# One VectorE chunk instead of two in the layer norms of the first and last layers of an attention and FP4 feed-forward stack, with a new planned order

## The chip, the cores and the metric

The kernel runs on one core of a Trainium2 chip. The metric is device time in microseconds (us) for one execution, and smaller is better. The five engines of the core run side by side and meet at semaphores: TensorE (PE; the weight loads are shown apart as PEld), VectorE (DVE), ScalarE (ACT), GpSimd (POOL) and SyncE (SP), which issues the transfers. The reference is in float32 and so is every matmul of the kernel; a float32 matmul shows in the trace as two instructions.

## The reference

The input holds 8 batches of 1024 tokens with 128 features. Cut to what matters:

```python
mod = (silu(c) @ wmod).reshape(8, 6, 1, 128)         # sa, ca, ga, sb, cb, gb
h = layernorm(x) * (1 + ca) + sa
for i in range(6):                                   # DEPTH
    xn = layernorm(h, ln1_w[i], ln1_b[i])
    q, k, v = xn @ wq[i], xn @ wk[i], xn @ wv[i]     # 8 heads of 16
    q, k = softmax(q, over features), softmax(k, over tokens)
    h = q @ (k.T @ v) @ wo[i] + bo[i] + h
    xn = layernorm(h, ln2_w[i], ln2_b[i])
    h = leaky(xn @ w1[i], 0.01) @ w2[i] + h          # 128 -> 512 -> 128
x = x + ga * h
h = layernorm(x) * (1 + cb) + sb
gate, up = fp4(h) @ fp4(w_gate).T, fp4(h) @ fp4(w_up).T      # 352 wide
return x + gb * (fp4(silu(gate) * up) @ fp4(w_down).T)
```

`fp4` scales blocks of 16 by their largest magnitude and rounds them to a grid of eight magnitudes. There are thus 2 layer norms in each of 6 layers for each of 8 batches, and 2 more for each batch around them.

## The kernel before

**Tiling.** One batch is a tile of 128 partitions by 1024 columns: 8 chunks of 128 columns, each holding 128 tokens. Nearly every step works on a half (H = 2) of HC = 4 chunks. There are four lanes of buffers (LANES = 4). Batch b uses lane b % 4, so batches 0 to 3 start the kernel together and batches 4 to 7 follow as the lanes come free.

**A half layer norm** (`layernorm`, called once for each half) is this chain. DVE takes `bn_stats` of four chunks (line 641) and aggregates them (647). ACT takes a logarithm and an exponential (661, 666) for a first reciprocal root. DVE refines it and makes the shift in four small steps (671 to 687). Then the four chunks are normalised: DVE does HV chunks (`apply_v`, line 693: one subtract and multiply each) and ACT the other HC - HV (`apply_s`, line 700: one activation each). HV is 2 in all norms within the layers. PE then transposes the four chunks (line 719) and ACT moves the result out of PSUM with the norm's weight and bias (929). In tile names, `a` marks the norm ahead of the attention, `m` the one ahead of the 512 wide part, `i` the one ahead of the first layer and `f` the one ahead of the FP4 part. Both `i` and `f` are made by `modulated_norm`, which passes its own HV.

**The rest of a layer.** k matmuls (949) with a maximum on DVE (956) and exponentials on ACT (972); q matmuls (996) with softmax steps on DVE, ACT and POOL (1005 to 1037); transposes; the 128 by 128 context (1059 to 1100); the output matmuls (1126), added onto x by DVE (1111); then the `m` norm, the first wide matmul (1172), Prelu on ACT (1181) and the second wide matmul (1189). After six layers `ffn` makes the FP4 rounding (747 to 792), gate and up matmuls (1233), silu on ACT (1241), the product on DVE (1249), and `down` rounds that, transposes it (1289), multiplies (1313), adds onto x (1322) and stores.

**The order.** Nothing is issued in the order in which it is written. `add` puts each step into a list with its engine, its modelled duration, and what it reads and writes; from these come the dependences. `Plan.order` then plays the list through a model of the engines and of the 8 PSUM banks. At each turn it takes the step that can start soonest; among equals, the one with the longest modelled tail plus a lead. Leads come from `LEAD[b][i]` (batch b, stage i: 0 is the start, 1 to 6 the layers, 7 the FP4 part), and `TURNS` replaces single leads when the model's clock passes a given time. The resulting order is fixed on every engine, which takes its instructions one after another.

**Fillers.** Where the model sees PE idle for longer than GAP (0.35 us), it puts in 128 by 128 matmuls of the identity into a free bank (`warm`, line 1361) until BRINK (0.1 us) ahead of the next step. Until the model's time COLD (11.5 us) PE's work counts double, `mm(P)` being 0.223 us otherwise:

```python
cold = 2 if e == "PE" and free[e] < self.COLD else 1
gap = e == "PE" and t - free[e] > self.GAP / cold
while gap and min(bank_free) <= free[e]:
    to = free[e] + cold * mm(P)
    if to > t - self.BRINK:
        break
```

Of the kernel before, what the change touches and what calls it, by code (L numbers as in the profile page):

```python
# [14 lines left out]
P = 128  # L15
# [47 lines left out]
class Ps:  # L63


    n = 0
# [17 lines left out]
class Plan:  # L84
# [58 lines left out]
    def order(self, leads, turns, warm):  # L143


        steps = self.steps
        for s in steps:
            for d in s.deps:
                steps[d].outs.append(s.n)
        for s in reversed(steps):  # L150
            s.tail = s.occ + s.lat + max((steps[o].tail for o in s.outs), default=0.0)
        free = dict.fromkeys(self.LAT, 0.0)
        free["PE"] = 1.8
        bank_free = [0.0] * BANKS
        left = [len(s.deps) for s in steps]
        ready = [0.0] * len(steps)
        cand = {e: {s.n for s in steps if s.eng == e and not s.deps} for e in free}
        table, port_free, now = None, 0.0, 0.0
        leads, turns = [list(x) for x in leads], list(turns)
        out, todo = [], len(steps)  # L160
        while todo:
            while turns and turns[0][0] <= now:
                for b, i, lead in turns.pop(0)[1]:
                    leads[b][i] = lead
            banks = sorted(bank_free)
            best = None
            for e, c in cand.items():
                for n in c:
                    s = steps[n]
                    t = max(free[e], ready[n], port_free if s.port else 0.0)  # L170
                    need = sum(x.bank is None for x in s.ps)
                    if need:
                        t = max(t, banks[need - 1])
                    if t < INF:
                        cost = SWITCH if s.func and table and s.func != table else 0.0


                        lead = leads[s.stage[0]][s.stage[1]] if s.stage else s.lead
                        pick = (t + cost, -s.tail - lead, n, t, cost)
                        if best is None or pick < best[1]:  # L180
                            best = (e, pick)
            assert best is not None
            e, (_, _, n, t, cost) = best
            cold = 2 if e == "PE" and free[e] < self.COLD else 1
            gap = e == "PE" and t - free[e] > self.GAP / cold
            while gap and min(bank_free) <= free[e]:
                to = free[e] + cold * mm(P)
                if to > t - self.BRINK:
                    break
                w, bank = Step(), bank_free.index(min(bank_free))  # L190
                w.fn, w.func = lambda bank=bank: warm(bank), None
                free[e] = bank_free[bank] = to
                out.append(w)
            s, todo = steps[n], todo - 1
            cand[e].discard(n)
            now = t + cost
            end = now + s.occ * (2 if e == "PE" and now < self.COLD else 1)
            table = s.func or table
            port_free = end if s.port else port_free
            for x in s.ps:  # L200
                if x.bank is None:
                    x.bank = min(range(BANKS), key=lambda i: bank_free[i])
                    bank_free[x.bank] = INF
                x.users -= 1
                if x.users == 0:
                    bank_free[x.bank] = end + s.lat
            free[e] = end
            for o in s.outs:
                ready[o] = max(ready[o], end + s.lat + self.SEE[steps[o].eng])
                left[o] -= 1  # L210
                if left[o] == 0:
                    cand[steps[o].eng].add(o)
            out.append(s)
        return out
# [21 lines left out]
def mm(n):  # L236

    return 0.0115 + n * 1.654e-3
# [11 lines left out]
def kernel(  # L250
# [22 lines left out]
    B, T, D = x_d.shape  # L273
# [15 lines left out]


    LEAD = [
        [2405, 3996, 461, 247, -1202, -1296, -1300, -3196],
        [1413, 1593, 3441, 1928, -2207, 1189, 1781, -248],
        [366, -108, -1676, -2703, -3835, 1594, -2630, -2514],
        [-241, 558, -1413, 208, -413, 228, -5405, -156],
        [694, -3633, -2192, -2384, -870, -487, -1194, -1272],
        [-3687, 2479, 1403, 3083, -1193, -6, -811, -1034],
        [725, 1777, 204, -1637, -400, -327, -320, -670],
        [3404, 589, 1158, 1867, -7, -962, -419, -2719],
    ]  # L300

    TURNS = [
        (3, [(1, 0, -62)]),
        (27, [(3, 0, -535)]),
        (36, [(2, 1, -485)]),
        (39, [(3, 1, -531)]),
        (45, [(0, 2, 1516), (2, 1, -553)]),
        (48, [(2, 1, -544)]),
        (57, [(1, 1, 1518), (1, 2, 2846), (1, 3, 649)]),
        (75, [(1, 1, 1516)]),  # L310
        (90, [(1, 1, 773)]),
        (105, [(0, 3, 2919), (0, 4, 1470), (0, 5, 1376), (0, 7, -524)]),
        (120, [(0, 3, 2762), (2, 1, -721)]),
        (150, [(1, 2, -201)]),
        (165, [(2, 1, 797)]),
        (180, [(1, 2, 1215)]),
        (210, [(2, 2, 832)]),
        (225, [(3, 1, 914), (3, 6, -4315)]),
        (240, [(0, 5, 828)]),
        (255, [(0, 5, 2639), (0, 6, 2635)]),  # L320
        (270, [(2, 3, 156)]),
        (285, [(0, 7, 811), (1, 3, 64)]),
        (300, [(4, 0, -33)]),
        (315, [(2, 2, 1013), (4, 0, 939)]),
        (330, [(3, 2, 544)]),
        (345, [(0, 7, 348), (2, 3, -400)]),
        (360, [(0, 7, 811), (2, 3, 1746), (2, 4, -2375)]),
        (405, [(1, 4, -3784), (4, 1, -3690)]),
        (420, [(1, 4, -3786)]),
        (435, [(2, 4, -3941)]),  # L330
        (450, [(1, 4, -2313)]),
        (465, [(4, 1, -4514)]),
        (480, [(1, 5, 1477)]),
        (495, [(3, 5, 1525)]),
        (525, [(1, 5, 1515), (2, 5, 1254)]),
        (555, [(1, 7, 1337)]),
        (570, [(2, 5, 1311)]),
        (600, [(1, 7, 1342)]),
        (615, [(1, 7, 1337), (3, 6, -3519), (5, 2, 2464)]),
        (630, [(3, 7, 1425)]),  # L340
        (675, [(5, 1, 2181)]),
        (690, [(4, 1, -2521)]),
        (705, [(2, 7, -2804), (4, 2, -2786), (4, 3, -4487), (4, 7, -1958)]),
        (735, [(5, 2, 3162)]),
        (780, [(6, 1, 323)]),
        (795, [(2, 7, -2027)]),
        (810, [(3, 7, 2088), (5, 3, 1769)]),
        (825, [(4, 3, -2043)]),
        (840, [(5, 4, -2386), (7, 1, 210), (7, 2, 779)]),
        (870, [(4, 3, -2494)]),  # L350
        (885, [(7, 1, 493)]),
        (915, [(6, 2, 913)]),
        (930, [(4, 3, -1826), (4, 4, -1241)]),
        (945, [(5, 4, -2139), (5, 6, -1878)]),
        (975, [(6, 3, -2917)]),
        (1005, [(7, 4, -2167)]),
        (1020, [(5, 5, -1207)]),
        (1035, [(5, 5, -1166)]),
        (1065, [(7, 4, -1977)]),
        (1140, [(4, 6, -2161), (5, 6, -1912)]),  # L360
        (1155, [(4, 6, -1857)]),
        (1170, [(4, 7, -1928)]),
        (1245, [(5, 7, -1905)]),
        (1260, [(6, 7, -139)]),
        (1275, [(6, 6, -1635)]),
        (1305, [(5, 7, -1974), (7, 7, 205)]),
        (1320, [(6, 7, -143), (7, 6, -143)]),
        (1335, [(6, 7, 201)]),
        (1350, [(6, 7, 206), (7, 7, 207)]),
    ]  # L370
    LATE = 140.0
    NQ = 4
# [252 lines left out]
    def layernorm(ln, dst, src, h, n, HV=HC // 2):  # L625
# [72 lines left out]
        def apply_s():  # L698
# [6 lines left out]
        low, high = at(dst, h)  # L705
        add(
            "ACT", (HC - HV) * (act(D, 2) + 0.04), apply_s, r=[*at(src, h), shift, rstd],
            w=[high] if HV else [low, high],
        )
        if HV:  # L710
            add("DVE", HV * 0.256, apply_v, r=[*at(src, h), mv, rstd], w=[low], port=True)
# [205 lines left out]
            )  # L917


    def normed(ln, x, which, to, l, params, n):  # L920


        xh, xT = big(ln, which, f"xh_{n}"), big(ln, to, f"xT_{n}")
        for h in range(H):
            layernorm(ln, xh, x, h, n)
            t = transposed(xh, h)
            add(
                "ACT", act(HW, 2),
                lambda t=t, h=h: nc.scalar.activation(  # L929
                    half(xT, h), t.ap(), AF.Identity,  # L930
                    bias=col(params + 1, l), scale=col(params, l),
                ),
                r=[t, "cols"], w=at(xT, h),
            )
        return xh, xT

    def layer(x, b, l, ln, mod):
        n = f"{b}_{l}"
        xh, xT = normed(ln, x, "A", "B", l, 0, f"a{n}")

        nmax = Buf(lanes_p, [P, H + 1], f"nmax{ln}", f"nmax_{n}", H + 1)
        ksum = Buf(lanes_p, [P, H + 1], f"ksum{ln}", f"ksum_{n}", H + 1)
# [188 lines left out]
            add("PE", HC * mm(D), out_mm, r=[*at(qT, h), m], w=[to])  # L1131
            onto_x(to, h)

        _, xmT = normed(ln, x, "C", "A", l, 2, f"m{n}")
        if l == L - 1:


# [283 lines left out]
```

## Time and profile before

| | |
|---|---|
| median of 3 runs | 1401.61 us (1401.01 to 1402.49) |
| the profiled execution's own time | 1401.35 us |
| its span, first to last instruction | 1399.6 us |
| PE busy | 1387.0 us, 99% of the span; 21.0 us of it fillers |
| DVE busy | 1136.8 us, 81% |
| ACT busy | 967.7 us, 69% |
| POOL busy | 250.3 us, 18% |

The profile is one execution. The span leaves out what lies ahead of the first and behind the last instruction: 1401.35 - 1399.6 = 1.75 us. A busy PE includes fillers, which are there only because nothing else could run. The gap that matters is therefore PE's idle time and its fillers together: 1399.6 - 1387.0 + 21.0 = 33.6 us.

### The profile page before, as it was taken

The page shows a single profiled execution, that of the slowest core. Times are in us where ns is not written, and L with a number is a line of the kernel's source. Part 1 is how long each engine was busy: PE and PEld are TensorE (multiplying, and loading weights), DVE is VectorE, ACT ScalarE, POOL GpSimd, SP SyncE. Part 2 cuts the span into 40 slices and gives each one's busy share as a digit, 9 for nine tenths or more (in the row PEclk, how much of TensorE's full clock was granted, in tenths as well). Part 3 has the DMA queues.
Part 4 walks back from the last instruction along what each step waited for, and adds up shares of the span by engine and source line. Part 5 has one row for each costly group of instructions (what it writes and reads, how often), then busy time and mean ns, then how long its engine had stood idle before and what let it go on. Part 6 is the DMA issues. An engine that isn't in the chain of part 4 may idle for free. (4 is left out here: it accounts for less than half of the span.)

```text
span 1399.6 us, 26260 instructions
## 1 busy us (share of the span) xinstructions
PE 1387.0 (99%) x9149; PEld 1112.8 (80%) x9149; DVE 1136.8 (81%) x4504; ACT 967.7 (69%) x2284; POOL 250.3 (18%) x216
## 2 busy tenths in 40 slices
PE   8999999999999999999999999999999999999999
PEld 6779778877888887877787788787877887888877
DVE  8998747689878674999899999685767576899997
ACT  6786756676777765777768767676667667677674
POOL 2312000022201010223121241011011022222332
PEclk9999999999999999999999999999999999999999
DMA  7100000000000000000000000000000000000001
GB/s 219 48 1 1 1 1 1 1 17 12 16 1 1 1 1 1 16 13 18 30 12 13 0 31 1 1 1 1 1 1 1 1 1 1 2 1 1 16 8 38
DMA packets 16436, 18.77 MB, mean 13 GB/s; under 512 B 1600, under 2 KB 10536, under 8 KB 16304
## 3 DMA queue, kind: packets, MB, share of 16 engines
q1 hardware_dynamic: 16304, 17.10, 4.0%
q8 instruction: 72, 1.18, 0.4%
q14 instruction: 60, 0.49, 0.1%
HBM read 12.88 MB, written 4.22 MB: 12 GB/s over the span
## 5 line engine op out<-in xcount | busy, mean ns | idle before, releaser
L1172 PE MATMUL ps<-xT_m,w_sb 128*128 128x512 f32 x768 | 351.5, 593 | 1.3 <-ACT g L1241 0.9
L1172 PEld LDWEIGHTS ps<-xT_m,w_sb 128*128 128x128 f32 x768 | 136.3, 190 | 126.5 <-issue 90.4
L1037 POOL TENSOR_TENSOR q<-q,qsum 128x512 f32<-128x512 f32 x96 | 101.7, 1070 | 703.0 <-DVE qsum L1032 312.8
L1111 DVE TENSOR_TENSOR x<-ps,x 128x512 f32<-128x512 f32 x192 | 130.4, 683 | 111.8 <-PE ps L1189 96.5
L996 PEld LDWEIGHTS ps<-wq_sb,xT_a 128*128 128x128 f32 x768 | 96.3, 192 | 26.1 <-issue 16.5
L700 ACT ACTIVATE xh_a<-x,shift_a,rstd_a 128x128 f32<-128x128 f32 x192 | 83.3, 488 | 26.0 <-DVE shift_a L687 25.6
L1189 PEld LDWEIGHTS ps<-w_sb,hT_D 128*128 128x128 f32 x640 | 86.8, 192 | 15.8 <-issue 13.2
L996 PE MATMUL ps<-wq_sb,xT_a 128*128 128x128 f32 x768 | 98.6, 275 | 0.0
L1189 PE MATMUL ps<-w_sb,hT_E 128*128 128x128 f32 x640 | 97.6, 275 | 0.0
L1189 PE MATMUL ps<-w_sb,hT_C 128*128 128x128 f32 x640 | 97.6, 275 | 0.0
L1189 PE MATMUL ps<-w_sb,hT_B 128*128 128x128 f32 x640 | 97.6, 275 | 0.0
L1189 PE MATMUL ps<-w_sb,hT_D 128*128 128x128 f32 x640 | 97.5, 275 | 0.0
L949 PE MATMUL ps<-xT_a,wk_sb 128*128 128x512 f32 x192 | 96.9, 604 | 0.3 <-DVE stats_a L641 0.3
L1126 PEld LDWEIGHTS ps<-m,qT 128*128 128x128 f32 x768 | 91.4, 192 | 6.4 <-issue 1.4
L1059 PEld LDWEIGHTS ps<-k,xh_a 128*128 128x128 f32 x768 | 90.7, 192 | 6.4 <-issue 4.3
L1126 PE MATMUL ps<-m,qT 128*128 128x128 f32 x768 | 94.9, 275 | 0.0
L1059 PE MATMUL ps<-k,xh_a 128*128 128x128 f32 x768 | 93.4, 275 | 0.0
L700 ACT ACTIVATE xh_m<-x,shift_m,rstd_m 128x128 f32<-128x128 f32 x192 | 81.3, 487 | 17.3 <-DVE shift_m L687 17.2
L661 ACT ACTIVATE rstd_a<-mv_a,eps 128x4 f32<-128x4 f32 x96 | 28.4, 299 | 92.2 <-DVE mv_a L647 79.6
L641 DVE BATCH_NORM_STATS2 stats_a<-x 128x6 f32<-128x128 f32 x384 | 85.2, 279 | 1.6
L929 ACT ACTIVATE xT_m<-ps,cols 128x512 f32<-128x512 f32 x96 | 72.4, 777 | 19.9 <-PE ps L719 19.6
L641 DVE BATCH_NORM_STATS2 stats_m<-x 128x6 f32<-128x128 f32 x384 | 84.7, 280 | 0.4
(181 smaller groups left out, 3217.5 us busy)
## 6 DMA issues: line engine op xcount, KB each, us to landing
x<-in_L_attn_x_dram SPq DMA_DIRECT2D x16, 256.0 KB, 3.0
out_dram<-x SPq DMA_DIRECT2D x14, 256.0 KB, 2.0
w_sb<-in_L_attn_w_dram SPq DMA_DIRECT2D x12, 256.0 KB, 4.6
mod<-mod_d SPq DMA_DIRECT2D x8, 256.0 KB
mod<-mod_d SPq DMA_DIRECT2D x4, 128.0 KB
out_dram<-x SPq DMA_DIRECT2D x4, 128.0 KB, 1.8
wk_sb<-in_L_attn_wk_dram SPq DMA_DIRECT2D x6, 64.0 KB, 3.9
wq_sb<-in_L_attn_wq_dram SPq DMA_DIRECT2D x6, 64.0 KB, 3.6
```

The lines of the kernel that those rows point to most:

```text
L641: "DVE", 0.197, lambda c=c: nc.vector.bn_stats(stats.ap()[:, c, :], s(c)),
L661: lambda: nc.scalar.activation(y(), var(), AF.Ln, bias=eps),
L700: nc.scalar.activation(d(c), s(c), AF.Identity, bias=shift.ap()[:, c : c + 1], scale=rstd.ap()[:, c : c + 1],)
L929: lambda t=t, h=h: nc.scalar.activation(half(xT, h), t.ap(), AF.Identity, bias=col(params + 1, l), scale=col(params, l),),
L949: lambda tk=tk, h=h: nc.tensor.matmul(tk.ap(), wk_sb[:, l, :], half(xT, h), start=True, stop=True),
L996: nc.tensor.matmul(tq.ap()[:, c * D : (c + 1) * D], half(xT, h)[:, c * P : (c + 1) * P], wq_sb[:, l, :], start=True, stop=True,)
L1037: lambda h=h, hs=hs: nc.gpsimd.tensor_tensor(heads(half(q, h)), heads(half(q, h)), each(qsum.ap()[:, hs]), ALU.mult),
L1059: nc.tensor.matmul(tc_.ap()[:, :D], chunks(xh.ap())[:, c, :], chunks(k.ap())[:, c, :], start=(c == 0), stop=(c == C - 1),)
L1111: lambda: nc.vector.tensor_tensor(half(x, h), t.ap(), half(x, h), ALU.add),
L1126: nc.tensor.matmul(to.ap()[:, c * D : (c + 1) * D], half(qT, h)[:, c * P : (c + 1) * P], m.ap(), start=True, stop=True,)
L1172: lambda th=th, h=h, j=j: nc.tensor.matmul(th.ap(), w1_sb[:, l, j * P : (j + 1) * P], half(xmT, h), start=True, stop=True,),
L1189: nc.tensor.matmul(ty.ap()[:, c * D : (c + 1) * D], hidden(j)[:, c * P : (c + 1) * P], w2g.ap()[:, j, :] if l == L - 1 else w2_sb[:, l, j, :],
```

## The change

Three things are edited.

1. `normed` and `layernorm` get HV from `layer`: 1 instead of 2 in the first layer (l = 0) of batches 0 to 3 and in the last (l = 5) of batches 6 and 7. In the other layers it stays 2, and the modulated norms are as before. Where HV is not HC // 2, ACT's step is also booked as a writer of the half's `low` part, in which DVE's chunk lies.
2. In `Plan.order` the doubling is no longer settled once for a gap; each filler is counted double or single by the model's time at which it starts. The threshold of a gap is GAP throughout.
3. `LEAD` has new values in nearly every place, and `TURNS` is a new list.

```diff
-            cold = 2 if e == "PE" and free[e] < self.COLD else 1
-            gap = e == "PE" and t - free[e] > self.GAP / cold
+            gap = e == "PE" and t - free[e] > self.GAP
             while gap and min(bank_free) <= free[e]:
-                to = free[e] + cold * mm(P)
+                to = free[e] + mm(P) * (2 if free[e] < self.COLD else 1)
                 if to > t - self.BRINK:
                     break
...
     LEAD = [
-        [2405, 3996, 461, 247, -1202, -1296, -1300, -3196],
-        [1413, 1593, 3441, 1928, -2207, 1189, 1781, -248],
...
+        [2558, 3947, 443, 241, -1194, -1097, -1236, -3189],
+        [1976, 2610, 4383, 2929, -1168, 2060, 2788, 764],
...
     TURNS = [
-        (3, [(1, 0, -62)]),
-        (27, [(3, 0, -535)]),
...
+        (9, [(2, 0, 2687)]),
+        (15, [(1, 0, -208)]),
...
             "ACT", (HC - HV) * (act(D, 2) + 0.04), apply_s, r=[*at(src, h), shift, rstd],
-            w=[high] if HV else [low, high],
+            w=[high] if HV == HC // 2 else [low, high],
         )
         if HV:
             add("DVE", HV * 0.256, apply_v, r=[*at(src, h), mv, rstd], w=[low], port=True)
...
-    def normed(ln, x, which, to, l, params, n):
+    def normed(ln, x, which, to, l, params, n, hv):
...
-            layernorm(ln, xh, x, h, n)
+            layernorm(ln, xh, x, h, n, hv)
...
     def layer(x, b, l, ln, mod):
         n = f"{b}_{l}"
-        xh, xT = normed(ln, x, "A", "B", l, 0, f"a{n}")
+
+        ends = b < LANES and l == 0 or b >= B - 2 and l == L - 1
+        hv = HC // 4 if ends else HC // 2
+        xh, xT = normed(ln, x, "A", "B", l, 0, f"a{n}", hv)
...
-        _, xmT = normed(ln, x, "C", "A", l, 2, f"m{n}")
+        _, xmT = normed(ln, x, "C", "A", l, 2, f"m{n}", hv)
```

## Prediction

> **What bounds the kernel now.** I read the page's busy times first, then the groups of PE for the fillers, then the windows by stage, and last the timelines of both ends.
>
> ```profile
> span 1399.6 us, 26260 instructions
> PE 1387.0 (99%) x9149; PEld 1112.8 (80%) x9149; DVE 1136.8 (81%) x4504; ACT 967.7 (69%) x2284; POOL 250.3 (18%) x216
> L1361 PE MATMUL warm<-ident 128*128 128x128 f32 x142 | 21.0, 291 | 1.6 <-POOL ident masks.py:199 1.6
> ```
>
> TensorE is busy 99%, but 21.0 us of it are fillers. Its needed work is 1387.0 - 21.0 = 1366.0 us and the gap (idle and fillers) 33.6 us. The change touches none of the needed matmuls, so it can only move those 33.6 us. The stages show where they are:
>
> ```profile
> core 0: us, PE busy (x) PEld busy (x) DVE busy (x) ACT busy (x) POOL busy (x), PEclk, DMA share, GB/s
> 10.00:16.00 6.00, 4.70 (x41) 4.48 (x41) 6.00 (x41) 2.92 (x12) 2.87 (x2) 1.00 0.98 304
> 16.00:46.00 30.00, 26.91 (x179) 21.73 (x179) 29.64 (x143) 21.60 (x66) 6.05 (x5) 0.94 0.68 188
> 46.00:100.00 54.00, 54.00 (x345) 41.97 (x345) 52.97 (x249) 44.08 (x112) 14.24 (x12) 1.00 0.01 1
> 100.00:1250.00 1150.00, 1148.38 (x7617) 922.42 (x7616) 907.76 (x3650) 792.36 (x1863) 182.65 (x153) 1.00 0.02 6
> 1250.00:1300.00 50.00, 50.00 (x306) 38.55 (x305) 47.06 (x167) 39.99 (x85) 11.84 (x10) 1.00 0.00 1
> 1300.00:1330.00 30.00, 30.00 (x221) 26.00 (x220) 27.50 (x94) 20.02 (x49) 8.21 (x7) 1.00 0.05 19
> 1330.00:1362.00 32.00, 30.81 (x195) 24.00 (x194) 30.77 (x75) 23.28 (x48) 10.95 (x7) 1.00 0.03 9
> 1362.00:1381.00 19.00, 18.98 (x116) 15.19 (x114) 17.04 (x34) 11.66 (x24) 6.91 (x5) 1.00 0.08 28
> 1381.00:1400.00 19.00, 15.46 (x126) 14.19 (x123) 13.13 (x34) 5.60 (x16) 4.07 (x4) 1.00 0.12 42
> ```
>
> From 46 to 1330 us PE is full but for 1.6 us, and without a filler; nothing is to be won there. The gap lies at the ends: up to 46 us, 12.0 us of fillers and 6.6 idle; from 1330, 9.0 us of fillers and 4.4 idle. At both ends DVE has next to no room: 35.64 of 36 us from 10 to 46, and 47.06 + 27.50 + 30.77 + 17.04 = 122.4 of 131 us from 1250 to 1381. ACT has room: 24.5 of 36, and 94.95 of 131. So at the ends DVE decides when PE gets work. What the edited instructions cost:
>
> ```profile
> L700 ACT ACTIVATE xh_a<-x,shift_a,rstd_a 128x128 f32<-128x128 f32 x192 | 83.3, 488 | 26.0 <-DVE shift_a L687 25.6
> L693 DVE TENSOR_SCALAR xh_a<-x,mv_a,rstd_a 128x128 f32<-128x128 f32 x192 | 61.7, 365 | 0.0
> ```
>
> And the first norm of batch 0, with PE's fillers ahead of it:
>
> ```profile
> 9.95 4.51 PE L1361 MATMUL warm<-ident 128*128 128x128 f32 x38
> 15.28 0.60 DVE L693 TENSOR_SCALAR xh_a<-x,mv_a,rstd_a 128x128 f32<-128x128 f32 x2
> 15.46 0.88 ACT L700 ACTIVATE xh_a<-x,shift_a,rstd_a 128x128 f32<-128x128 f32 x2
> 15.76 0.95 PE L719 MATMUL ps<-ident,xh_a 128*128 128x128 f32 x4 [1.30 <-DVE xh_a L693]
> 17.14 0.95 PE L719 MATMUL ps<-ident,xh_a 128*128 128x128 f32 x4 [0.43 <-DVE xh_a L693]
> ...
> 20.00:21.00 1.00, 1.00 (x2) 0.48 (x3) 1.00 (x7) 1.00 (x3) 0.00 (x0) 0.50 0.46 92
> ```
>
> The fillers end at 14.46, PE idles 1.30, works in bits, and the granted clock (the last column but two of the window) is then half from about 19.4 to 22.7 us.
>
> **Chunks moved to ACT, price of one.** Two chunks in a row take 0.60 us on DVE and four 1.10 (the `m` norm at 42.78), so one more costs 0.25. On ACT two take 0.88 and four 1.65 (at 35.06), so one more costs 0.39. The change moves one chunk in each of 2 halves x 2 norms x 6 batches = 24 half norms: DVE -6.0 us, ACT +9.4 us. In the middle both are idle time exchanged.
>
> The Trainium skill speaks against this move: "ScalarE: Activation LUTs", section Rules for kernel authors, says to do an add or a multiply on VectorE and not on ScalarE. By that rule the move is a loss; with the two prices above it would be 24 x 0.14 = 3.4 us, an estimate that holds only if both engines were equally short of time. The windows decide: DVE is short at the ends and ACT is not.
>
> **Chunks moved, the latency.** ACT now books the `low` part too, and DVE's chunk is written into the same part behind it. In the plan, DVE's chunk therefore waits until ACT has done its three, and DVE gets it later in its fixed order even where the chip would not make it wait. At 15.28 to 16.34 the two engines worked side by side. With three on ACT, ACT ends 0.39 later (16.73), and DVE's single chunk behind that ends about 0.3 to 0.4 after it: 17.1, or 0.8 us later than now. If DVE in fact runs its chunk where it has always been, the delay is 0.4. Queued behind the ACT step are the next half's chunks and the copies out of PSUM (line 929); PE's transposes wait for both.
>
> **Start.** Before 46 us there are six half norms of the first layer: `a` at 15.28, 16.65, 34.90 and 35.48, and a pair of `m` at 42.78. DVE wins 6 x 0.25 = 1.5 us. The first `a` norm is on the path that gives PE its first real work; its delay, 0.4 to 0.8, comes once for the two halves, since the second starts 0.25 earlier and queues behind the first. The `m` norm at 42.78 adds the same again if nothing covers it; q work of the next batch stands beside it. Ends: -1.5 (latency hidden) and +1.6 - 1.5 = +0.1 (nothing hidden). I take -0.5, since PE has other lanes' work from 36 us on. The ten later half norms of batches 0 to 3 (53 to 106 us) are beside a full PE and count nothing; if that cover went, their ACT time would be 10 x 0.39 = 3.9 us.
>
> **Fillers.** The new threshold does nothing by itself: a cold filler needs 0.446 + 0.1 us of room, more than 0.175 or 0.35. What matters is the run of 19 fillers (38 instructions) from 9.95. The plan counted each at 0.446, 8.5 us in all, while they took 0.237 each. Those past 11.5 in the plan now count 0.223, so the same planned hole takes more. If the plan has the transposes ready when the chip had them (15.7), its hole runs from about 7 to 15.6 (my estimate): ten cold ones and 18 others, 28 in all, ending at 9.95 + 28 x 0.237 = 16.6. That is 0.85 us after the transposes could start (15.76), but closes the hole that came ahead of the half clock. The half clock made the four k instructions at 19.76 last until 23.00, 3.24 us, against 1.72 in the later rows: 1.5 us more. Ends: -1.5 (clock kept, new order leaves no overrun) and +0.85 (overrun, clock no better). I take both effects together, 0.85 - 1.5, about -0.7.
>
> The row on the clock and the skill differ: "TensorE: Matmul & The Clock Gate", the part on the HAM clock gate, has the clock fall after a whole idle window of about 3.4 us. Here the longest idle bit was 1.30 us in a stretch half busy (2.6 of 4.9 us), and the clock fell all the same. By the page the extra fillers would win nothing, and this term would be +0.85 instead of -0.7.
>
> **End.** Eight half norms (batches 6 and 7, last layer) leave DVE 8 x 0.25 = 2.0 us and give ACT 3.1 us in some 100 us where it is busy 72%. DVE is 93% busy from 1250 to 1381, so most of 2.0 us, not all, arrives at the tail, where fillers take 9.0 us. Against it stands the latency of up to 0.8 us of the last `m` norm (1328.34 and 1335.11). Ends: -2.0 and +0.8. I take -1.2: 93% of 2.0 is 1.9, less most of one latency.
>
> **New leads.** They change no duration. They fix who fits where, for which no row has a price: 1.6 us of idle in the middle bound the gain there, the 13.4 us at the end and the 18.6 at the start bound it at the ends. From below, the transfers and the first norm hold the first 10 us, and the store the last 2.9. From above, a planned wait that the chip does not keep costs what the present idle bits do, 0.3 to 1.3 us each, and four or five of them are 4 us. I take 0 and keep -2 and +4 for the range.
>
> **Sum.** -0.5 - 0.7 - 1.2 = -2.4 us against the profiled 1401.35 gives 1398.95. The median of the runs is 0.26 above that execution, so 1399.2.
>
> **Rivals.**
> - *Everything arrives.* Latencies hidden and clock kept: -1.5 - 1.5 - 2.0 = -5.0, so 1396.6. For it: DVE at 99% until 46. Against: the plan's ordering of DVE's chunk behind ACT's.
> - *DVE's time is not what is short.* Batch 0's chain (norm, k, maximum, exponential, q, context) sets the start, and the FP4 chain the tail; one chunk saved goes into work that nobody waits for. Then 1401 to 1402. For it: 2.9 us of fillers at 24.7 to 28.9 stand in batch 0's chain with DVE on other batches. The same time results if the edit changes nothing that the chip notices, the fillers merely replacing idle bits.
> - *ACT becomes the bound (slower).* Place: 46 to 106 us and 1250 to 1336, where ACT frees PSUM banks for PE. A three chunk step holds ACT 1.27 us instead of 0.88, and the copies and Prelu steps queue behind it. If all 24 reached PE it would be 24 x 0.39 = 9.4 us. Against: ACT 82% and 72% busy there. It decides from the point where a third of it, 3.1 us, reaches PE with no relief in return: 1401.6 + 3.1 = 1404.7; at half of it 1406.3.
>
> **Chances.** The forecast has 0.46 and its own range 1397.4 to 1401; everything arrives 0.20; no change 0.18; slower 0.16. About 0.2% of the time, 2.8 us, is what a measurement of this kernel can tell from no change: faster is below 1398.8, slower above 1404.4. The forecast's part below 1398.8 is 0.19 and with the first rival faster has 0.39; same has 0.27 + 0.18 = 0.45; slower 0.16. The range runs from 1395.8 (the first rival with a little from the leads) to 1404.8 (the slower rival at its threshold), with some 2 in 10 outside.
>
> **What would show it.** Right: in the changed profile, 24 fewer line 693 and 24 more line 700 instructions in the first 110 and last 150 us; the run of fillers after 9.95 longer than 38 and the clock near 1.00 in 16 to 46 us; fillers and idle under 17 us up to 46 us, and under 12.5 from 1330; the middle still with under 3 us idle. Wrong: PE waiting for ACT at lines 719, 949 or 1172 between 46 and 1330 us; the clock still at half somewhere before 46; the tail after the last line 1233 matmul (1380.9 now) as long as now and no earlier; or a gain that lies in the middle, where I see none.

## The result and the profile after

The changed kernel takes 1404.65 us (median of 16 runs, 1403.47 to 1405.36), the kernel before 1401.29 in 16 runs of the same sessions (1400.43 to 1402.72). The ratio is 1.0023 with a 95% interval of 1.0017 to 1.003: it is slower by 3.4 us, where 1399.2 was predicted. Line numbers from 693 on are higher by 10 to 13 in the changed file: 693 is now 703, 700 is 710, 719 is 729, 1172 is 1185, 1361 is 1374.

The head of the page and the groups of the fillers and of ACT's share of the `a` norms:

```profile
span 1403.0 us, 26357 instructions
PE 1391.4 (99%) x9195; PEld 1116.7 (80%) x9195; DVE 1126.4 (80%) x4480; ACT 986.4 (70%) x2316; POOL 248.6 (18%) x216
L1374 PE MATMUL warm<-ident 128*128 128x128 f32 x188 | 26.6, 284 | 1.6 <-POOL ident masks.py:199 1.6
L710 ACT ACTIVATE xh_a<-x,shift_a,rstd_a 128x128 f32<-128x128 f32 x204 | 87.8, 486 | 34.6 <-DVE shift_a L697 32.1
```

DVE is 10.4 us less busy and has 24 instructions fewer: the chunks did move. ACT is 18.7 us more busy, and the 24 chunks account for only about half of that (24 x 0.39 = 9.4). The rest comes with the order. Each time ACT passes from the silu of an FP4 part to an exponential or back, the program loads another table of functions, 1.28 us each time. There are now 29 such loads in place of 21, 10.3 us more in all. The loads of the two lines that grew, after and then before:

```profile
L1385 ACT ACT_TABLE_LOAD x14 | 18.0, 1283 | 0.2
L1254 ACT ACT_TABLE_LOAD x14 | 18.0, 1283 | 0.3
```

```profile
L1372 ACT ACT_TABLE_LOAD x10 | 12.8, 1283 | 0.2
L1241 ACT ACT_TABLE_LOAD x10 | 12.8, 1283 | 0.2
```

PE's needed work is 1391.4 - 26.6 = 1364.8 us, 1.2 less than before, which is about what the half clock at the start cost. Idle time and fillers, however, are 1403.0 - 1364.8 = 38.2 us against 33.6. So 4.6 us of new gap less 1.2 of work make the 3.4. The windows by stage (same columns as before):

```profile
10.00:16.00 6.00, 6.00 (x54) 5.92 (x54) 6.00 (x38) 2.92 (x13) 2.88 (x2) 1.00 0.95 306
16.00:46.00 30.00, 27.54 (x194) 22.90 (x193) 30.00 (x159) 26.31 (x76) 6.92 (x6) 1.00 0.63 190
600.00:900.00 300.00, 297.35 (x1927) 235.17 (x1926) 269.88 (x1005) 215.41 (x497) 71.50 (x56) 1.00 0.05 15
1330.00:1362.00 32.00, 31.40 (x186) 23.87 (x185) 30.46 (x82) 24.39 (x49) 9.81 (x7) 1.00 0.03 10
1362.00:1381.00 19.00, 18.97 (x133) 16.30 (x132) 16.44 (x37) 12.97 (x27) 5.09 (x4) 1.00 0.15 56
1381.00:1404.00 23.00, 19.02 (x138) 16.44 (x137) 16.23 (x41) 7.63 (x20) 5.97 (x5) 0.96 0.07 24
```

The same middle window of before reads:

```profile
600.00:900.00 300.00, 299.25 (x1958) 239.24 (x1957) 271.93 (x1024) 219.83 (x513) 70.85 (x55) 1.00 0.04 14
```

The start runs at clock 1.00 now (0.94 before). The largest piece of new idle time stands from 600 to 900 us, where no chunk was moved at all: 2.65 us against 0.75.

The clock at the start differs from execution to execution of before. Of the 68 executions that were timed beside the runs below, 9 show a mean clock of 1.000 and take 1400.42 us (median); the other 59, at 0.997 to 0.999, take 1401.56. All 16 of the changed kernel show 1.000. Against before with its clock kept, the change is thus 4.2 us slower.

Busy windows hide the rest, because the ends of matmuls are modelled and a short wait disappears in a longer busy bar. A second measure does not: the **lag** of PE at an instruction, which is its start less the work of all needed matmuls ahead of it at the back-to-back rate of their kind (7.14 us for 64 instructions of 128 columns, 6.87 for 16 of 512). The lag grows only where PE waits, runs a filler or has a slow clock. (The rates are a little high, so where nothing waits it falls, by 0.1 to 0.3 us in 100, in both kernels alike.) In us, by the work done (the chip's time of a mark is work plus lag):

| work done | 81 | 281 | 581 | 681 | 761 | 781 | 881 | 1281 | end |
|---|---|---|---|---|---|---|---|---|---|
| before | 24.11 | 24.06 | 25.14 | 25.49 | 25.77 | 25.69 | 26.93 | 26.71 | 40.81 |
| after | 22.75 | 22.28 | 21.51 | 24.25 | 24.18 | 27.29 | 27.98 | 29.19 | 44.16 |

After the start, at some 100 us of the run, the changed kernel is 1.36 us ahead, and at 600 it is 3.6 ahead. From about 600 to 900 it loses 6.5 us (before 1.8), from there to 1300 1.2 (before -0.2), and in the tail 15.0 (before 14.1). Against before that is -1.36, -2.27, +4.68, +1.43 and +0.87: 3.35 us in all, the difference of the spans.

The stretch from 600 to 900 us is where batches 0 to 3 end with their FP4 part and batches 4 to 7 are in full work. PE's waits there, after:

```profile
PE ps L729 <- DVE xh_m L703: 1.0, 1, 1.0
PE ps L729 <- POOL h L802: 0.4, 1, 0.4
PE ps L1106 <- DVE ctxT L1098: 0.4, 1, 0.4
PE ps L962 <- ACT xT_a L939: 0.3, 1, 0.3
```

And before:

```profile
PE ps L1233 <- ACT g L1241: 0.4, 1, 0.4
PE ps L949 <- DVE stats_a L641: 0.3, 1, 0.3
```

After, the longest is a wait for DVE, for a chunk of an `m` norm. The timeline (start, length, engine, tiles, and in brackets the idle time before it) shows what held DVE:

```profile
788.99 1.27 POOL L922 TENSOR_TENSOR h<-h,mod 128x512 f32<-128x512 f32 x1 [1.29 <-DVE shift_i L681]
789.02 1.25 DVE L681 SCALAR_TENSOR_TENSOR shift_m<-mv_m,rstd_m 128x4 f32<-128x4 f32 x1
791.07 0.15 DVE L681 SCALAR_TENSOR_TENSOR shift_m<-mv_m,rstd_m 128x4 f32<-128x4 f32 x1
791.22 1.41 POOL L802 TENSOR_TENSOR g<-fv_g,scale_g 128x704 f32<-128x704 f32 x1 [0.96 <-DVE shift_m L681]
791.29 1.35 DVE L686 SCALAR_TENSOR_TENSOR shift_m<-shift_m,rstd_m 128x4 f32<-128x4 f32 x1
792.86 0.59 DVE L703 TENSOR_SCALAR xh_m<-x,mv_m,rstd_m 128x128 f32<-128x128 f32 x2
793.25 1.75 PE L729 MATMUL ps<-ident,xh_m 128*128 128x128 f32 x8 [1.02 <-DVE xh_m L703]
```

A refinement step on 128 by 4 values takes 0.15 us when it runs alone (791.07) and 1.25 or 1.35 us when it starts within 0.1 us of a large GpSimd step; both end together. DVE is 19.96 of 20 us busy from 780 to 800, against 18.95 before, and PE waits 1.02 us. At this instruction alone the lag jumps by 1.18 us, and from 785 to 808 us it grows by 3.1.

Neither a full DVE nor the stretching is new by itself. Before, DVE is just as full from 800 to 840, and PE hardly waits:

```profile
800.00:820.00 20.00, 19.95 (x139) 16.67 (x138) 19.98 (x56) 14.40 (x32) 3.39 (x2) 1.00 0.07 27
820.00:840.00 20.00, 20.00 (x135) 15.70 (x134) 19.93 (x67) 13.86 (x36) 11.38 (x8) 1.00 0.07 27
```

And from 600 to 900 us 17 DVE steps take over 0.2 us more than the median of their kind, in either kernel: 12.3 us more together before, 14.7 after. So it must matter what other work PE has at hand when such a step comes; that is argued and not shown.

At the end, after and then before, the first transpose of the last FP4 half and the last `down` matmuls:

```profile
1384.37 0.82 PE L1302 MATMUL ps<-ident,g 128*128 128x128 f32 x6
...
1399.15 0.94 PE L1326 MATMUL ps<-wdb,gT 128*128 128x128 f32 x6
```

```profile
1380.74 0.82 PE L1289 MATMUL ps<-ident,g 128*128 128x128 f32 x6
...
1395.79 0.93 PE L1313 MATMUL ps<-wdb,gT 128*128 128x128 f32 x6
```

That chain is 14.78 us long after and 15.05 before. It merely starts 3.63 us later.

### The profile page after: what moved, and what is told of

It reads as the page before. It is cut to its first block, busy times and chain, and to the rows that moved or that the text cites. A ratio compares the mean times of both kernels' runs of the same rounds, so it can differ in the third digit from the quotient of the medians.

```text
span 1403.0 us, 26357 instructions
## 1 busy us (share of the span) xinstructions
PE 1391.4 (99%) x9195; PEld 1116.7 (80%) x9195; DVE 1126.4 (80%) x4480; ACT 986.4 (70%) x2316; POOL 248.6 (18%) x216
## 4 chain that ended last, share of the span: by engine, by line
PE 89%; DVE 7%; ACT 3%; issue 0%; DMA 0%; SPq 0%; POOL 0%; DVEq 0%
PE ps L1185 22%; PE ps L1202 21%; PE ps L729 11%; PE ps L1072 6%; PE ps L1009 6%; PE ps L1139 6%; PE ps L962 6%; PE ps L1246 5%; PE ps L1326 3%; PE ps L1302 1%; DVE x L1124 1%; PE ps L1106 1%; PE ps L1081 1%; PE warm L1374 1%; DVE stats_m L651 1%; DVE stats_a L651 1%
## 5 line engine op out<-in xcount | busy, mean ns | idle before, releaser
L710 ACT ACTIVATE xh_a<-x,shift_a,rstd_a 128x128 f32<-128x128 f32 x204 | 87.8, 486 | 34.6 <-DVE shift_a L697 32.1
L710 ACT ACTIVATE xh_m<-x,shift_m,rstd_m 128x128 f32<-128x128 f32 x204 | 85.7, 486 | 18.8 <-DVE shift_m L697 18.6
L1202 PEld LDWEIGHTS ps<-w_sb,hT_D 128*128 128x128 f32 x640 | 86.6, 192 | 14.1 <-issue 11.0
L939 ACT ACTIVATE xT_a<-ps,cols 128x512 f32<-128x512 f32 x96 | 72.6, 777 | 20.4 <-PE ps L729 20.0
L1202 PEld LDWEIGHTS ps<-w_sb,hT_B 128*128 128x128 f32 x640 | 84.5, 192 | 0.7 <-issue 0.5
```

Source lines behind the costliest of these rows:

```text
L710: nc.scalar.activation(d(c), s(c), AF.Identity, bias=shift.ap()[:, c : c + 1], scale=rstd.ap()[:, c : c + 1],)
L939: lambda t=t, h=h: nc.scalar.activation(half(xT, h), t.ap(), AF.Identity, bias=col(params + 1, l), scale=col(params, l),),
L1202: nc.tensor.matmul(ty.ap()[:, c * D : (c + 1) * D], hidden(j)[:, c * P : (c + 1) * P], w2g.ap()[:, j, :] if l == L - 1 else w2_sb[:, l, j, :],
```

## The experiments

My theory was that the **order** is to blame: the new leads pack the stages so that a wait reaches PE where DVE has nothing to spare, and the edits at the ends are worth little either way. The rivals were that the **chunks** on ACT cost the time, and that the **fillers** overrun. "Slip" is the difference of the start of the same PE instruction in the profiles of two kernels that have the same order. Executions of one order differ at the start for no reason in the edits (at 100 us a_light, a_short and a_mid stand at -0.90, +0.34 and +0.48 against the change), so slips are read as steps between stages, and at the start only beside the medians. Edits shift line numbers in the views of a run by a few: a_light's 1107 is 1106 of the change. All medians stand beside runs of before at 1401.3 to 1401.6 us.

### The filler counting alone: c_fill

Before, with edit 2 only; PE's order of real work stays, and the long run has 35 fillers instead of 19.

```diff
-            cold = 2 if e == "PE" and free[e] < self.COLD else 1
-            gap = e == "PE" and t - free[e] > self.GAP / cold
+            gap = e == "PE" and t - free[e] > self.GAP
...
-                to = free[e] + cold * mm(P)
+                to = free[e] + mm(P) * (2 if free[e] < self.COLD else 1)
```

> The kernel before with the new way of counting fillers alone. Its order is that of before on every engine; only the run of fillers ahead of batch 0's first transposes grows, from 19 to 35. Theory 'order' (the loss sits in the new leads, the fillers are worth little): 1400.5 to 1402.5 us against 1401.3. Theory 'fillers' (the longer run holds back the transposes): 35 fillers of 0.237 us end at 9.95 + 8.3 = 18.2, 2.5 us after the chunks are ready, less the half clock that goes (1.5): 1402.3 or more. If the half clock were all that counts: 1399.8.

Measured: 1400.58 us, ratio 0.9994 (0.9985 to 1.0003). The window of the start:

```profile
16.00:46.00 30.00, 26.94 (x193) 22.61 (x192) 30.00 (x145) 23.15 (x69) 6.12 (x5) 1.00 0.65 190
```

The clock stays at 1.00. The first transposes come 1.46 us later, at 17.22, because the fillers overrun, and at 25 us everything is 1.3 us earlier; 0.74 of that lasts to the end. The medians differ by 0.7 as well, inside their interval. All 11 executions show clock 1.000, and their median is within 0.2 us of the 1400.42 of before with its clock kept: what the fillers are worth is the clock.

### The change without the filler counting: g_hv_leads

```diff
-            gap = e == "PE" and t - free[e] > self.GAP
+            cold = 2 if e == "PE" and free[e] < self.COLD else 1
+            gap = e == "PE" and t - free[e] > self.GAP / cold
...
-                to = free[e] + mm(P) * (2 if free[e] < self.COLD else 1)
+                to = free[e] + cold * mm(P)
```

> The changed kernel with the old way of counting fillers. Its order is that of after; only the long run shrinks from 30 to 17 fillers and ends at about 14.1 us, 3.7 us ahead of the first transposes. Theory 'order': the hole brings the half clock back, 1404.65 + 0.5 to 1.5 = 1405.2 to 1406.2. Theory 'fillers' (the new fillers cost the time): 1402 to 1403.5.

Measured: 1406.5, ratio 1.0038 (1.0025 to 1.0051), 1.85 above the full change. PE's first transposes and the window:

```profile
17.70 0.89 PE L730 MATMUL ps<-ident,xh_a 128*128 128x128 f32 x4 [3.99 <-DVE mv_i L658]
16.00:46.00 30.00, 26.68 (x181) 22.67 (x182) 29.30 (x146) 24.75 (x73) 5.97 (x5) 0.94 0.67 192
```

With 17 fillers in the long run instead of 30, PE is idle for 3.99 us and the clock falls to half for a while again. So the counting helps in the new order, and in the old one by as much as c_fill shows; the loss is not there. The gap in the middle is as in the full change.

### Two chunks on DVE in the new order: a_two

The plan is that of the change, to the last place; only the ranges of the two steps differ, so that DVE does two chunks and ACT two in all norms.

```diff
-            for c in range(HV):
+            for c in range((HV or 0) and 2):
...
-            for c in range(HV, HC):
+            for c in range((HV or 0) and 2, HC):
```

> The changed kernel in its own order on every engine, but VectorE does two chunks in every layer norm, as before; ScalarE does the other two. Theory 'order': within 1.2 us of 1404.65, and PE's gap from 600 to 900 us still 2 to 3 us. Theory 'chunks' (the chunk moved to ScalarE and queued behind it is what costs): ACT's step is 0.39 us shorter in 24 half norms; the time falls to 1402.5 or less.

Measured: 1407.53, ratio 1.0044 (1.0031 to 1.0058): 2.9 above the change, more than either theory allowed. The slip against the change is 1.53 at 46 us and 2.40 at 100, then stays at 2.6. In this order the single chunk is worth 2.9 us, nearly all of it at the start; it is not what costs the time. At equal chunks and the same filler counting the two orders now stand at 1407.5 (a_two) and 1400.6 (c_fill): the new order by itself is 6.9 us worse, with the booking of DVE's chunk behind ACT's that belongs to its plan. Some 1.8 of that has come by 100 us (lag 22.75 + 2.40 against 24.11 - 0.73), and the single chunk hides it in the change.

### One chunk on DVE in the old order: b_one

```diff
-            for c in range(HV):
+            for c in range(DV):
...
-            for c in range(HV, HC):
+            for c in range(DV, HC):
...
+        ends = b < LANES and l == 0 or b >= B - 2 and l == L - 1
+        dv = HC // 4 if ends else HC // 2
```

> The kernel before in its own order on every engine, but VectorE does one chunk in the layer norms of the first layer of batches 0 to 3 and the last of 6 and 7, beside ScalarE's three. Theory 'order': 1400.5 to 1402.2. Theory 'chunks': 1402.5 or more. If VectorE's time at the ends is what is short, as the prediction had it, 1398 to 1400.

Measured: 1402.06, ratio 1.0006 (0.9997 to 1.0014). The slip against before is 0.63 us by 100 us, none from there to 1250, 0.17 more from 1250 to 1300, and none behind that. The 0.63 is too small a price: this profile has the clock at 1.00 from 16 to 46 us, where that of before has 0.94. Against c_fill and b_28 (the last but one of these runs), which keep the clock in the old order, b_one stands 1.4 and 1.0 us later at 100 us; and its five executions at clock 1.000 have a median of 1401.70, 1.3 over the 1400.42 of before. In the old order the chunk at the start thus costs about 1 us, and the one at the end gives nothing, although DVE is 93% busy there.

### One chunk on DVE in the middle instead: a_mid

The order of the change, with every norm planned from 600 to 900 us at one chunk on DVE and three on ACT, to take DVE's load off where PE waits for it.

```diff
-            for c in range(HV):
+            for c in range(DV()):
...
+        def DV():
+            return min(HV, 1) if 600 <= plan.steps[k].at < 900 else HV
```

> The changed kernel in its own order on every engine, but in all layer norms that the plan has at 600 to 900 us VectorE does one chunk and ScalarE three. Theory 'DVE load' (PE's new waits at 640 to 690 and 785 to 820 us are VectorE's backlog where it is 100% busy): each such half norm gives VectorE 0.25 us back, and PE's waits of 5 us there shrink by 1 to 3 us: 1401.5 to 1403.7. Rival 'port' (they come from VectorE's small steps being held by GpSimd): within 0.6 us of 1404.65. Rival 'latency' (ScalarE's longer step counts): 1405 or more.

Measured: 1409.68, ratio 1.0056 (1.0042 to 1.0071), 5.0 above the change, which is a miss. The slip is 2.1 from 600 to 700, 1.1 more by 800 and 1.3 more by 1000. PE's waits from 600 to 900:

```profile
PE ps L734 <- DVE xh_m L703: 1.0, 1, 1.0
PE ps L967 <- ACT xT_a L944: 0.6, 1, 0.6
PE ps L734 <- ACT kT L990: 0.6, 1, 0.6
```

Line 734 here is 729 of the change, 967 is 962 and 990 is 985. The wait for DVE stays and two for ACT join it. The run does not test DVE's load cleanly, since it puts the same work onto another engine of the chain. It does price moved chunks in the middle, at 4.5 us by the slip; the two waits for ACT are 1.2 of that, and the rest has no shown cause.

### DVE's chunk beside ACT's three: a_beside

The change, with DVE's single chunk put in DVE's order to where ACT's step starts, instead of behind it.

```diff
+    for s in [s for s in steps if hasattr(s, "beside")]:
+        steps.remove(s)
+        steps.insert(steps.index(s.beside), s)
```

> The changed kernel; only VectorE's single chunk of the 24 edited half norms moves in VectorE's order from behind ScalarE's three chunks to right beside them. The other engines' orders stay. Theory 'latency': each of these half norms is ready 0.3 to 0.4 us earlier; the first transposes start at 17.4 instead of 17.8, and the time falls by 0.5 to 1.5 us, 1403.2 to 1404.2. Theory 'order': within 0.5 us of 1404.65, for the middle decides.

Measured: 1406.58, ratio 1.0035 (1.0022 to 1.0048), 1.9 above the change: a miss for both theories. The first transposes do come 0.44 us earlier, but the slip rises from 0.59 to 1.80 between 46 and 100 us, and by 0.4 more after 1300. The chunk's later place is not the harm. That the steps which it pushes back on DVE matter more is only argued.

### A shorter GpSimd step: a_short

The order of the change; GpSimd's last FP4 multiply (line 802) does the first 64 columns only, where it is planned from 640 to 830 us. The other columns are left out.

```diff
+            n = 4 if last == "POOL" and 640 <= plan.steps[k].at < 830 else nb
...
-            lambda: eng.tensor_tensor(blocks(src()), blocks(vv()), each(s()), ALU.mult),
+            lambda: scaled(),
```

> The changed kernel in its own order, but GpSimd's last multiplication of the FP4 rounding handles only the first 64 columns where the plan has it at 640 to 830 us; the rest of that product is left out. It frees no VectorE instruction; it takes away most of the time in which GpSimd can hold VectorE there, and makes that step some 1.2 us shorter for those who wait for it. Theory 'port': the stretched VectorE steps of 600 to 900 us fall from 14 to half and the time to 1400 to 1403. Theory 'DVE load': 1403.5 to 1404.7.

Measured: 1403.19, ratio 1.001 (1.0001 to 1.0019), 1.5 under the change and between the ranges of the two theories. The slip falls by 1.8 between 600 and 800 us and is flat from 100 to 600 and behind 800. By the count above, 14 DVE steps are stretched from 600 to 900 instead of 17, far from half. The largest piece, 1.09 us, falls at the wait of 793.25: the step that took 1.35 us there takes 0.26 beside the short GpSimd step. Another 0.58 falls at 649.79, where PE waited for GpSimd's own product. GpSimd's steps are part of the loss.

### Less work for DVE in the handover, in both orders: a_light and b_light

The second FP4 rounding step on DVE (line 794, 784 before) does 64 columns where it is planned from 640 to 830 us, the rest being left out. That takes 8.1 us (14 steps) off DVE in the new order and 7.2 us (12 steps) in the old one, and gives nobody else work. If the new order lets DVE's backlog through to PE and the old one covers it, the first gains much more than the second.

```diff
+            n = 64 if 640 <= plan.steps[k].at < 830 else ncol
+            a, b = v.ap()[:, :n], mag.ap()[:, :n]
+            nc.vector.scalar_tensor_tensor(a, b, ROUND, a, ALU.max, ALU.subtract)
```

> The changed kernel in its own order, but the second rounding step of the FP4 part handles only its first 64 columns where the plan has it at 640 to 830 us; the rest of that step is left out. It takes 8.1 us of VectorE's time away there (14 steps), adds none to ScalarE and lengthens no chain. Theory 'slack' (the new order has VectorE planned without a gap at the second handover, so each of its steps that runs longer than planned reaches PE): 1399.2 to 1402.2. Theory 'port' (only the holding by GpSimd counts, as in the run with short GpSimd steps): 1402.8 to 1404. Theory 'ScalarE' (its chain is the late one, as the run with one chunk in the middle could mean): 1404 to 1405.

> The control to it: the kernel before in its own order, with the same step left out beyond 64 columns where its plan has it at 640 to 830 us (12 steps, 7.2 us of VectorE's time). Theory 'slack': the order of before has planned gaps on VectorE that take up most of what runs longer, so PE gets at most what it waits there now: 1400.3 to 1401.4, a fall of 1 us at most. If VectorE's load is what both orders pay for there, it falls by 2 us or more, to 1399.3 or less.

Measured: a_light 1401.54, ratio 0.9997 (0.9988 to 1.0006), 3.1 under the change; b_light 1400.58, ratio 0.9991 (0.9983 to 1.0), 1.0 under the runs of before beside it (1401.56). The slip of a_light falls by 3.2 us between 600 and 800 (-0.90 to -4.09) and by nothing after; that of b_light by 0.3 up to 800 and 0.7 more by 1000. From 600 to 900 us a_light loses 3.3 us of lag where the change loses 6.5; the jumps of 1.18 and 0.58 us at 793.25 and 649.79 are the two largest of the change, and neither is left over 0.21. The gain of a_light lies in two places: 1.5 us from 649.8 to 653.9 us and 1.7 from 793.2 to 794.7. PE's longest waits in a_light from 600 to 900, and its window where the change reads `14.96` for DVE and `13.93` for PE:

```profile
PE ps L1107 <- DVE ctxT L1099: 0.4, 1, 0.4
PE ps L963 <- ACT xT_a L940: 0.3, 1, 0.3
PE ps L729 <- DVE xh_m L703: 0.2, 1, 0.2
```

```profile
785.00:800.00 15.00, 14.60 (x103) 11.62 (x102) 13.44 (x60) 9.68 (x27) 3.94 (x3) 1.00 0.05 19
```

The wait of 1.0 us at line 729 is down to 0.2. From nearly the same relief the new order gains 3.2 us and the old one 1.0 (0.3 of it up to 800 us). So in the new order more of DVE's work reaches PE. In the first of the two places this is not quite separated: the shortened step also lies in the FP4 chain for which PE waits at 649.79 (0.37 us of the gain) and 653.46 (0.46). In the second place PE waits for a norm, in which the shortened step has no part.

### How many fillers keep the clock: b_24 and b_28

Before, with 24 or 28 fillers in place of the 19 of the long run.

```diff
+    steps[first : first + 19] = (steps[first : first + 19] * 2)[: 24]
```

> The kernel before with 24 fillers in the long run instead of 19; nothing else. They end at 9.95 + 24 x 0.237 = 15.6, just ahead of the first transposes. Theory 'clock' (the fillers' worth is the half clock alone): 1399.6 to 1400.3, below the 1400.6 of the run of 35, which overran. If the overrun of 35 cost nothing because VectorE or ScalarE was the later one: 1400.3 to 1400.9. If 24 do not keep the clock: 1401 to 1401.6.

> The kernel before with 28 fillers in the long run (19 before, 24 and 35 tried). They end at 9.95 + 28 x 0.237 = 16.6, 0.8 us after the first chunks are ready. If closing the hole ahead of the transposes keeps the clock: 1399.8 to 1400.8. If it takes more than that, as 24 did: 1401 to 1402.

Measured: b_24 1401.41, ratio 0.9999 (0.999 to 1.0008); b_28 1400.56, ratio 0.9993 (0.9984 to 1.0002). Four microseconds of b_24, then the start of b_28:

```profile
15.00:16.00 1.00, 0.48 (x4) 0.18 (x3) 1.00 (x8) 0.86 (x4) 0.00 (x0) 1.00 1.07 323
18.00:19.00 1.00, 0.45 (x3) 0.31 (x2) 1.00 (x14) 1.00 (x7) 0.00 (x0) 0.70 0.76 221
20.00:21.00 1.00, 1.00 (x4) 0.48 (x4) 1.00 (x8) 1.00 (x3) 0.00 (x0) 0.50 0.40 89
24.00:25.00 1.00, 1.00 (x6) 1.00 (x6) 0.48 (x1) 0.00 (x0) 0.72 (x1) 0.50 0.78 221
```

```profile
16.00:46.00 30.00, 26.03 (x181) 21.41 (x181) 30.00 (x146) 22.20 (x67) 6.19 (x5) 1.00 0.64 189
```

With 24 the hole of 1.30 us is gone and no idle bit exceeds 0.55 us. Yet PE is busy for only 2.5 of the 4 us from 15 to 19, and in this execution the clock is at half from 18.4 to 25.2 us. It is the slowest of the 11 (1402.70). Four others show clock 1.000 and take 1399.74 to 1400.98; the six left show 0.998 or 0.999 and take 1401.07 to 1402.64. So with 24 fillers the clock falls in most executions and not in all. With 28 all 11 show 1.000, at 1400.26 to 1400.95.

### The chunks alone, planned anew: d_hv

Edit 1 with the old leads and the old counting; one execution.

```diff
-            w=[high] if HV else [low, high],
+            w=[high] if HV == HC // 2 else [low, high],
...
-        xh, xT = normed(ln, x, "A", "B", l, 0, f"a{n}")
+        xh, xT = normed(ln, x, "A", "B", l, 0, f"a{n}", hv)
```

> The change of the chunks alone, planned anew with the leads of before and the old way of counting fillers. Theory 'leads' (a list of leads fits the one set of steps that it was made for): the order falls apart and PE gets many fillers; 1440 us or more. If the leads were robust: 1400 to 1404.

Measured: 1484.33 us, 345 fillers:

```profile
L1364 PE MATMUL warm<-ident 128*128 128x128 f32 x690 | 91.5, 279 | 1.6 <-POOL ident masks.py:199 1.6
```

Two changed durations and one more dependence in 24 of 192 half norms change the whole order, and with leads of the old steps that costs 83 us. By the lag, 41 of them are lost up to 800 us and 35 in the last 77 us of work. The part by itself cannot be judged by planning anew; a_two and b_one, which keep an order, are the usable tests of it.

## Why the prediction was wrong

**Start, chunks and fillers (-0.5 and -0.7): the sum right by luck, one part not.** Together -1.2; the lag at 100 us is 1.36 us smaller. The fillers' -0.7 is c_fill's -0.7, and -1.85 in the new order (g_hv_leads), where they do not overrun: they end at 17.04, PE waits 0.76 more, and the clock is kept. The chunks cost about 1 us in the old order (b_one) and are worth -2.4 by 100 us in the new one (a_two), not -0.5: I had priced them without asking in which order they would stand. The order's own loss at the start, some 1.8 us, made the sum come out. It is chance, too, that 24 x 0.14 = 3.4 us, the price of the moved chunks if all counted in full, is the measured loss: in the new order the chunks gain.

**Latency: right.** From the end of the shift step to the end of both shares it takes 17.66 - 15.89 = 1.77 us, against 16.34 - 15.36 = 0.98 before: 0.8 later, as worked out. PE's first transposes come 2.05 us later (17.81, before 15.76), for PE now waits for DVE's chunk, which comes last; but the first k matmuls start at 19.74, before at 19.76. DVE's chunk does run behind ACT's:

```profile
15.98 2.42 ACT L710 ACTIVATE xh_a<-x,shift_a,rstd_a 128x128 f32<-128x128 f32 x6
17.34 0.32 DVE L703 TENSOR_SCALAR xh_a<-x,mv_a,rstd_a 128x128 f32<-128x128 f32 x1
17.81 0.63 PE L729 MATMUL ps<-ident,xh_a 128*128 128x128 f32 x4 [0.76 <-DVE xh_a L703]
```

**End (-1.2): wrong.** I took DVE's 93% for a sign that its saved time would reach the tail. b_one shows a slip of +0.17 there and the change itself a lag of +0.9. A busy engine is not yet the engine that PE waits for: the chain of the last FP4 half keeps its length, 15.05 us before and 14.78 after, and starts later, which the prediction had named as a sign against it.

**New leads (0): the step that failed.** The text named the mechanism, a planned wait that the chip does not keep, and its +4, but took 0, since 1.6 us of idle time in the middle seemed to leave nothing to move there. That bounds neither side. Between the ends the change is, by the lag, -2.3 us from 100 to 600 (two of the moved chunks lie there, behind 140 us), +4.7 from 600 to 900, where none lies, and +1.4 from 900 to 1300 (two lie there, behind 1240): +3.8 in all, nearly all of it for a term that I put at 0. And leads do more than fix who fits where: these brought eight more table loads. The runs that change one thing at a time give the terms directly. The fillers are -0.7 (before to c_fill), the new order is +6.9 (c_fill to a_two), the chunks in it are -2.9 (a_two to the change); these three steps lead from 1401.30 to 1404.65 us. The prediction had -0.7, 0 and -1.7.

**The rivals.** "Everything arrives" and "DVE's time is not what is short" both missed. "ACT becomes the bound" had the right sign and a time near the result, but not its cause: in the change, no wait of PE between 600 and 900 for ACT is longer than 0.3 us, or 0.45 by the lag (at 804 us). That a wait of PE for ACT occurs there at all (line 962, 949 before) had been named as a sign of being wrong. Of the signs listed, the counts (two of the half norms only behind 140 us), the longer filler run and the clock came as said. Gap up to 46 us is 19.4 us and from 1330 14.7, over the 17 and 12.5 that I had set, and the middle's idle time 3.35, over the 3.

**The cause.** The new order costs the time: 6.9 us at equal chunks and equal filler counting. Part of how is shown. From 600 to 900 us, where the FP4 part of batches 0 to 3 meets the norms of 4 to 7, more of DVE's work, and of small steps that are stretched beside GpSimd, reaches PE. Of the 6.5 us lost there, 3.2 go when DVE is relieved and 1.8 when GpSimd's steps are shortened (the two overlap at 793 us), while the same relief of DVE gives the old order 1.0. So 2.2 of the 4.7 by which this stretch is worse go with the relieved step; it is some of DVE's work only, and up to 0.8 of the 2.2 may be the shorter FP4 chain instead. That DVE has nothing to spare does not tell the two orders apart, since in that of before it is just as full from 800 to 840 us. **Open:** the rest of that stretch, the +1.4 from 900 to 1300 and the +0.9 of the tail were not tested apart, and the 1.2 us of a_beside between 46 and 100 us has no shown cause. Nor were the eight table loads tested. From 600 to 900 us there are 10 against 8, and none starts in the 6 us ahead of a jump of the lag by more than 0.2 us, which speaks against them there; from 900 to 1300 there are 9 against 6, and behind that 6 against 3.

No version beats before beyond doubt. The best are c_fill and b_28, the old order with more fillers at the start, 0.7 and 1.0 us under it with intervals that just include 1. Executions of before that keep the clock by themselves are as fast.

## What to carry to other kernels

An order worked out against a model is one thing with the steps for which it was tuned: when it changes, do not put its price at zero because the middle looks full. Here one such stretch lost 4.7 us and another gained 2.3. Count what the order adds, too, such as table loads. To learn what an edit of a step is worth, keep the order fixed and change only what the step does; planned anew, the same edit gave +83 us. Time saved on an engine that is 93% busy counts only if the engine that sets the end is waiting for it.

## What the runs showed of the hardware

The clock fell to half after PE had been busy for 2.5 of 4 us, without any idle bit over 0.55 us (b_24's profile), and it did not do so every time: it was kept in 4 of 11 executions with 24 fillers in the long run, in 11 of 11 with 28, and in 9 of 68 with 19.

A GpSimd step can hold up a VectorE step until it ends: a 128 by 4 step of 0.15 us took 1.25 and 1.35 us beside GpSimd steps of 1.27 and 1.41 us. Of the steps of this size that took over 0.25 us, 25 before and 19 after, every one ended within 0.03 us behind the end of a GpSimd step.
